# Graph attention with edge features on one core: one 384-element iota of GpSimd behind each batch of gathers, or one 128-element iota behind each gather

## The chip, the cores and the metric

The kernel runs on one core of a Trainium2 chip. Times are device microseconds of one execution. Where a profile is read, times are counted from the first instruction of the profiled execution, and "the span" is the time from its first to its last instruction. The engines are TensorE (PE; its weight loads are shown apart as PEld), VectorE (DVE), ScalarE (ACT), GpSimd (POOL) and SyncE (SP). Only the SP, ACT and POOL queues issue DMAs here.

## The reference

A graph has 6250 nodes with 128 features each and 206250 directed edges (200000 of them drawn in both directions, plus one self loop for each node). The edges are sorted by their destination. Each edge has 128 features of its own.

```
Qh, Kh, Vh = h @ WQ, h @ WK, h @ WV          # (6250, 8 heads, 16)
Eh         = edge_attr @ WE                  # (206250, 8, 16)
score = sum over 16 of Kh[src] * Qh[dst] * Eh / 4
score = exp(clip(score, -5, 5))
msg   = Vh[src] * score
h_out = segment_sum(msg, dst) / (segment_sum(score, dst) + 1e-6)
out   = layernorm(x + h_out)
```

The part that matters here is `Kh[src]` and `Vh[src]`: for every edge a row of 256 floats (K and V side by side) has to be fetched by its source node, and sources come in no order.

## The kernel before, in words

**Tiles and batches.** The edges are cut into `NT` = 1612 tiles of 128 (the last is partly padding). `cut_batches` groups them in 406 batches: 401 batches of `B` = 4 tiles, then five small ones that hold the last eight tiles (2, 2, 2, 1, 1).

**The table and the gathers.** At the start, the kernel writes the table `kv` (6250 rows of 256 floats) to HBM: `table` multiplies the nodes by `wkv`. From then on, `gather` (L304 to L320) fetches, for each tile, one row of 256 floats for each of the 128 edges, with one indirect DMA that GpSimd issues (L311) into a slot of the buffer `kvrows`. There are `GB` = 16 such buffers, one for a batch. The first `XB` = 12 batches can't wait for the table: they gather raw node rows from `x` (48 gathers) and multiply them by `wkv` later (`project`). Batches 12 to 405 gather from `kv`: 389 batches of four and five small ones, 1564 gathers.

**What GpSimd does beside gathers.** Behind the gathers of each batch from 12 on, GpSimd writes a row of 384 integers in each partition of a tile called `pause` (L319). Nothing reads that tile. It occupies GpSimd between the gathers of one batch and those of the next. Three other iotas run once, at the start: `io_i` (L118, 384 elements), `io2` (L121, 128 elements) and `third` (L138, one element).

**What sets the order.** From batch 12 on the instructions keep the order in which they are written (`manual_schedule`, L465). Each engine works through its own queue in order. In one turn of the loop (L463) GpSimd gets the gathers of batch b. The other engines work on several batches at once, each a stage further on: PE expands Q from a window of rows to the edges (`stage_a`, L353, into `qps`) and multiplies the edge features by `we` (L357); DVE multiplies the two (`pairs`, L364); PE transposes the product (`turn`, L372, into `pps`); DVE multiplies it by the gathered K (`stage_b`, L378, into `kq`), sums over 16 features (L381) and clips (L384); ACT takes the exponential (`weigh`, L390, L392); DVE multiplies the gathered V by it (`messages`, L412); PE sums the messages by destination with a one-hot matrix (`stage_c`, L430). The one-hot matrices come from DVE (`stage_0`, L339 and L343).

**What a gather waits for.** The gather for tile t waits for the landing of the gather eight earlier (GpSimd's DMAs go round eight semaphores). The first gather of a batch also waits until its buffer is free, which is after `messages` of the batch 16 earlier. And from batch `LOCK` = 20 on, the first gather of batch b waits for Q's expansion of batch b - 2 (L314 to L317). That dependency is in both kernels.

Of the kernel before, what the change touches and what calls it, by code (L numbers as in the profile page):

```python
# [15 lines left out]
P = 128  # L16
# [12 lines left out]
XB = 12  # L29
# [51 lines left out]
def edge_attention(ctx: ExitStack, tc: tile.TileContext, x, xT, srcT, dstT, dstB, dst0, bnd, lo, eaT,  # L81
                   wq, wkv, we, out, kv, qtab, qs, relD):
    nc = tc.nc
# [25 lines left out]
    def src_col(t):  # L109
        return src_sb[0][:, t:t + 1] if t < C0 else src_sb[1][:, t - C0:t - C0 + 1]  # L110

    with ExitStack() as fast:
# [6 lines left out]
        pause = ip.tile([P, 3 * P], I32, name="pause")  # L119
# [184 lines left out]
        def gather(b):  # L304
            rows, f = (x, D) if b < XB else (kv, 2 * D)
            g = gp.tile([P, B, 2 * D], F32, name="kvrows")
            for i, t in enumerate(batches[b]):
                k = min(P, (E - t * P + 63) // 64 * 64)
                if k < P:
                    nc.vector.memset(g[k:, i, :], 0.0)  # L310
                ins = nc.gpsimd.indirect_dma_start(  # L311
                    out=g[:k, i, :f], out_offset=None, in_=rows,
                    in_offset=bass.IndirectOffsetOnAxis(ap=src_col(t)[:k], axis=0))
                if i == 0 and b >= LOCK:  # L314
                    tc.add_manual_dep(ins.ins, expanded[b - STEP].ins.name,
                                      mybir.DependencyInfo(mybir.DependencyClass.Sync, mybir.DependencyReason.DATA),
                                      reason="gathers keep to TensorE's pace")  # L317
            if b >= XB:
                nc.gpsimd.iota(pause, pattern=[[1, 3 * P]], base=0, channel_multiplier=0)  # L319
            return g  # L320

        def project(g, n):
# [94 lines left out]
        def stage_c(b):  # L417
            n, g, oh, m = st8.pop(b)
            for i in range(n):
# [18 lines left out]
                elif last:  # L438
# [3 lines left out]
                    if k[1] == 0 and k[0] > 0:  # L442
                        ready.append(k[0] - 1)

        gathered = {b: gather(b) for b in range(min(XB, len(batches)))}
        for b0 in range(0, NB, KB):
            table(b0)
# [15 lines left out]
        for b in range(nbat + 4):  # L463
# [6 lines left out]
            if b < nbat:  # L470
                load_chunk(batches[b][0] // CH + EB - 3)
                load_rel(batches[b][0] // RC + 1)
                load_q(batches[b][0] // WT + QLOOK)
                g = gathered.pop(b) if b in gathered else gather(b)
                if b == min(XB, nbat - 1):
                    late_loads()
                if b == min(XB + 8, nbat - 1):
                    relative(C0, NT)
                if b == 14:
                    from_window(1)  # L480
                if b == 0:
                    for i in range(AHEAD):
                        stage_0(i)
                if b > 0:
                    turn(b - 1)
                stage_a(b, g)
            elif b == nbat:
                turn(b - 1)
# [178 lines left out]
```

## Time and profile before

| | |
|---|---|
| median of three runs | 2204.58 us (2202.32, 2204.58, 2208.21) |
| profiled execution | 2208.21 us, with a span of 2206.3 us |
| PE busy | 1468.0 us (67% of the span) |
| DVE busy | 1626.8 us (74%) |
| ACT busy | 478.9 us (22%) |
| POOL busy | 1719.4 us (78%), 2013 instructions |
| DMA | 398.18 MB, 180 GB/s on average |
| mean granted TensorE clock | 0.866 |

The busy share of an engine counts the time in which one of its instructions is shown as executing. A gather's bar on POOL shows GpSimd at work on it, not the transfer: the data lands later, and its landing is seen in what DVE waits for. The time that passes between two instructions of an engine with nothing to wait for is called "issue" by the profile. It isn't counted as busy, but the engine can't do anything else in it. So an engine can be without a moment to spare at a busy share well below 100%, and the way to see it is to look at what its waits are, not at the share.

### The profile page before, as it was taken

How to read it: one execution, taken by the hardware profiler on the slowest of the kernel's cores; microseconds unless marked ns; L12 is line 12 of the kernel's file. 1: busy time of each engine (PE TensorE's matmuls, PEld its weight loads, DVE VectorE, ACT ScalarE, POOL GpSimd, SP SyncE). 2: the span in 40 equal slices, each digit the busy share in tenths (PEclk: the TensorE clock that was granted, in tenths of full speed). 3: DMA queues.
4: the chain of work that ended last, by engine and by line, in shares of the span. 5: the costliest groups of instructions: out<-in, count | busy, mean ns of one | idle time of the engine just before them, and what ended most of it. 6: DMA issues, size and time to landing. Idle time of an engine off the chain costs nothing.

```text
span 2206.3 us, 25324 instructions
## 1 busy us (share of the span) xinstructions
PE 1468.0 (67%) x6880; PEld 1026.4 (47%) x6880; DVE 1626.8 (74%) x3779; ACT 478.9 (22%) x1572; POOL 1719.4 (78%) x2013
## 2 busy tenths in 40 slices
PE   6976666676666666666666666666766666666665
PEld 4754444454444444444444444444444444444443
DVE  3797778677777777777776776777777777777776
ACT  2522222222222221222221221222222211221211
POOL 7737777877777787787777778778778777777876
PEclk9998888878888998888888898998898888887888
DMA  8746555665566556555666556556655566656552
GB/s 283 247 135 203 173 183 160 192 193 163 171 188 193 180 163 199 177 182 161 181 188 181 181 168 201 179 163 191 186 181 163 177 192 181 181 165 200 176 161 78
DMA packets 178486, 398.18 MB, mean 180 GB/s; under 512 B 61757, under 2 KB 87527, under 8 KB 178337
## 3 DMA queue, kind: packets, MB, share of 16 engines
q0 software_dynamic: 76592, 208.18, 31.8%
q1 hardware_dynamic: 100604, 187.38, 27.2%
q8 instruction: 57, 0.93, 0.2%
q10 hardware_dynamic: 1140, 0.93, 0.1%
q14 instruction: 93, 0.75, 0.1%
HBM read 381.54 MB, written 14.81 MB: 180 GB/s over the span
## 4 chain that ended last, share of the span: by engine, by line
POOL 42%; DMA 21%; DVE 15%; issue 14%; PE 7%; POOLq 0%; ACT 0%; DVEq 0%; ACTq 0%; SPq 0%
POOL kvrows L311 39%; DMA kvrows<-kv,src 20%; POOL pause L319 4%; DVE kq L378 4%; DVE sc L381 3%; PE agg L430 2%; DVE msg L412 2%; DVE onehot L339 2%; PE eps L357 2%; DVE onehotT L343 1%; PE kvps L333 1%; PE pps L372 1%; DVE eq L364 1%; DMA kv<-kvst 1%; DVE sc L384 1%
## 5 line engine op out<-in xcount | busy, mean ns | idle before, releaser
L311 POOL DMA_INDIRECT kvrows<-kv,src x1564 | 1487.1, 951 | 453.1 <-issue 384.8
L430 PE MATMUL agg<-msg,onehot 128*128 128x136 f32 x3224 | 542.5, 318 | 605.0 <-DVE msg L412 295.4
L430 PEld LDWEIGHTS agg<-msg,onehot 128*128 128x128 f32 x3224 | 479.3, 218 | 916.7 <-issue 768.9
L378 DVE TENSOR_TENSOR kq<-kvrows,pps 128x512 f32<-128x512 f32 x406 | 276.3, 680 | 472.6 <-DMA kvrows<-kv,src 468.5
L357 PE MATMUL eps<-ea,we_sb 128*128 128x512 f32 (+1 forms) x812 | 487.9, 686 | 0.7 <-ACT kvrows L334 0.7
L372 PE MATMUL pps<-shift,eq 128*128 128x128 f32 x1612 | 310.2, 324 | 98.3 <-DVE eq L364 85.9
L355 ACT COPY qT<-qps 128x512 f32<-128x512 f32 x406 | 236.7, 583 | 587.1 <-PE qps L353 586.8
L372 PEld LDWEIGHTS pps<-shift,eq 128*128 128x128 f32 x1612 | 214.2, 163 | 155.8 <-DVE eq L364 150.0
L364 DVE TENSOR_TENSOR eq<-qT,eps 128x512 f32<-128x512 f32 x406 | 272.4, 671 | 18.9 <-PE eps L357 16.2
L381 DVE TENSOR_REDUCE sc<-kq 128x32 f32<-128x512 f32 x406 | 276.0, 680 | 7.3
L390 ACT ACTIVATE bank<-sc 128x32 f32<-128x32 f32 x406 | 81.8, 201 | 918.5 <-DVE onehot L339 911.8
L412 DVE TENSOR_TENSOR msg<-kvrows,bank 128x512 f32<-128x512 f32 x406 | 274.5, 676 | 5.6 <-ACT bank L390 5.5
L339 DVE TENSOR_TENSOR onehot<-bank,dst_sb 128x512 f32<-128x512 f32 x406 | 275.4, 679 | 0.0
L357 PEld LDWEIGHTS eps<-ea,we_sb 128*128 128x128 f32 x812 | 186.4, 231 | 31.6 <-ACT kvrows L334 3.2
L343 DVE TENSOR_SCALAR onehotT<-relb,node 126x512 bf16<-126x512 bf16 x406 | 192.7, 476 | 6.4 <-DMA relb<-relD 5.7
L319 POOL IOTA pause<- 128x384 int32 x394 | 185.3, 470 | 2.9
L353 PE MATMUL qps<-onehotT,qw 126*128 126x512 bf16 x406 | 183.2, 451 | 0.7 <-ACT qT L355 0.7
L384 DVE TENSOR_SCALAR sc<-sc 128x32 f32<-128x32 f32 x406 | 89.0, 219 | 7.3
L392 ACT ACTIVATE msg<-sc 128x32 f32<-128x32 f32 x406 | 86.5, 213 | 0.0
L400 PEld LDWEIGHTS finps<-sum,shift 128*128 128x128 f32 x478 | 64.5, 195 | 26.1 <-issue 25.9
L400 PE MATMUL finps<-sum,shift 128*128 128x136 f32 x478 | 64.4, 282 | 0.0
L311 POOL DMA_INDIRECT kvrows<-x,src x48 | 46.0, 958 | 16.2 <-issue 14.0
(67 smaller groups left out, 528.5 us busy)
## 6 DMA issues: line engine op xcount, KB each, us to landing
ea<-eaT SPq DMA_DIRECT2D x201, 512.0 KB
relb<-relD SPq DMA_DIRECT2D x100, 504.0 KB
kvrows<-kv,src POOLq DMA_INDIRECT x1564, 2.8
qw<-qs SPq DMA_DIRECT2D x202, 31.5 KB
kv<-kvst SPq DMA_DIRECT2D x12, 512.0 KB
qs<-qst SPq DMA_DIRECT2D x48, 96.0 KB
xb<-x SPq DMA_DIRECT2D x48, 64.0 KB
out<-h SPq DMA_DIRECT2D x48, 64.0 KB
```

The lines of the kernel that those rows point to most:

```text
L311: ins = nc.gpsimd.indirect_dma_start(out=g[:k, i, :f], out_offset=None, in_=rows, in_offset=bass.IndirectOffsetOnAxis(ap=src_col(t)[:k], a ...
L319: nc.gpsimd.iota(pause, pattern=[[1, 3 * P]], base=0, channel_multiplier=0)
L339: nc.vector.tensor_tensor(oh[:, :n], iota_p[:, None, :].to_broadcast([P, n, P]), rel[:, t0:t0 + n, None].to_broadcast([P, n, P]), op=ALU.i ...
L343: nc.vector.tensor_scalar(ohT[:, :n * P], rels[t0 // RC][:, e0:e0 + n * P], node[:QROWS], None, op0=ALU.is_equal)
L355: nc.scalar.copy(qT[:, :n * P], pq[:, :n * P])
L357: nc.tensor.matmul(pe[:, :n * P], we_sb, ea_tiles(t0, n), start=True, stop=True)
L364: nc.vector.tensor_tensor(eq[:, :n * P], qT[:, :n * P], pe[:, :n * P], op=ALU.mult)
L372: nc.tensor.transpose(pp[:, i, :], eq[:, i * P:i * P + P], ident)
L378: nc.vector.tensor_tensor(t1[:, :n], g[:, :n, :D], pp[:, :n], op=ALU.mult)
L381: nc.vector.tensor_reduce(sc[:, :n], t1[:, :n].rearrange("p b (h d) -> p b h d", h=H), axis=AX.X, op=ALU.add)
L412: nc.vector.tensor_tensor(m[:, :n, :D].rearrange("p b (h d) -> p b h d", h=H), g[:, :n, D:].rearrange("p b (h d) -> p b h d", h=H), exp_p[ ...
L430: nc.tensor.matmul(aggs[k], oh[:, i, :], m[:, i, :], start=first and not final, stop=last)
```

## The change

The iota behind each batch is taken out. Behind each single gather, from batch 12 on, GpSimd writes 128 integers in each partition of the same tile. A batch of four so has four iotas of 128 elements (512 elements in all) instead of one of 384; the small batches at the end have one for each of their gathers. GpSimd executes 1564 iotas instead of 394.

```diff
                 if i == 0 and b >= LOCK:
                     tc.add_manual_dep(ins.ins, expanded[b - STEP].ins.name,
                                       mybir.DependencyInfo(mybir.DependencyClass.Sync, mybir.DependencyReason.DATA),
                                       reason="gathers keep to TensorE's pace")
-            if b >= XB:
-                nc.gpsimd.iota(pause, pattern=[[1, 3 * P]], base=0, channel_multiplier=0)
+                if b >= XB:
+                    nc.gpsimd.iota(pause[:, :P], pattern=[[1, P]], base=0, channel_multiplier=0)
             return g
```

The instructions of PE, DVE, ACT and SP, and their order, stay as they are. No DMA is added, removed or moved.

## The prediction

> **What bounds the kernel now.** I read the waits first, because busy shares mislead here: POOL is busy 78% of the span, DVE 74%, PE 67%, and none looks full. The list of who waited for whom, restricted to GpSimd, has its causes on the right and total, number and longest wait behind the colon:
>
> ```profile
> POOL kvrows L311 <- issue: 398.8, 1428, 0.3
> POOL kvrows L311 <- DVE sc L384: 37.7, 26, 32.9
> POOL kvrows L311 <- DVE onehotT L343: 6.0, 33, 0.3
> POOL kvrows L311 <- DMA kvrows<-kv,src: 2.5, 11, 0.3
> ```
>
> The reader is to see the last column. With one exception no gather was ever held up by more than 0.3 us, and 0.3 us is what lies between any two gathers. The many small entries that name DVE, PE or a DMA are that same gap under another name. The exception is one wait of 32.9 us. GpSimd has nothing else to wait for, so outside that wait it is the bound, in spite of its 78%: 1719.4 busy, 453.1 + 16.2 idle before gathers, and 32.9 of that is the one real wait.
>
> The timeline of GpSimd (start, duration, instruction; in brackets the idle time before it) shows the rhythm, two batches of it:
>
> ```profile
> 155.89 0.47 POOL L319 IOTA pause<- 128x384 int32 x1
> 156.52 0.95 POOL L311 DMA_INDIRECT kvrows<-kv,src  x1 [0.16 <-DVE sc L381]
> 157.77 0.94 POOL L311 DMA_INDIRECT kvrows<-kv,src  x1 [0.30 <-issue]
> 159.02 0.95 POOL L311 DMA_INDIRECT kvrows<-kv,src  x1 [0.30 <-issue]
> 160.28 0.95 POOL L311 DMA_INDIRECT kvrows<-kv,src  x1 [0.30 <-issue]
> 161.24 0.46 POOL L319 IOTA pause<- 128x384 int32 x1
> 161.86 0.95 POOL L311 DMA_INDIRECT kvrows<-kv,src  x1 [0.16 <-DVE onehotT L343]
> ```
>
> From one batch to the next (156.52 to 161.86) it is 5.34 us, and near the end, at 2121.81 to 2127.15, it is 5.34 us again. Elsewhere the other engines wait for it. In the list of waits, DVE's greatest is for gathered rows:
>
> ```profile
> DVE kq L378 <- DMA kvrows<-kv,src: 468.5, 243, 6.2
> ```
>
> The one real wait stands in the early timeline:
>
> ```profile
> 106.13 0.47 POOL L319 IOTA pause<- 128x384 int32 x1
> 139.53 0.95 POOL L311 DMA_INDIRECT kvrows<-kv,src  x1 [32.94 <-DVE sc L384]
> ```
>
> Counting the gathers, this is the first gather of batch 20, where the wait for Q's expansion of batch b - 2 begins. In PE's timeline the expansion of batch 18 ends 0.27 us before 139.53, so that expansion is what it waited for. From then on the expansions pull ahead of the gathers, by a median of 14.0 us, since DVE needs only some 4 of each 5.34 us (518.33 busy of the 700 us from 700 to 1400). The last gather ends at 2191.67, and 14.6 us of PE and DVE work follow to the end of the span. So the end is set by: 139.53, plus 1531 steps of GpSimd from gather to gather, plus 15.6 us from the last gather's start.
>
> **The change, part by part.** The same 1532 gathers (batches 20 to 405) stay on that path. What changes is what stands between them.
>
> *What goes:* between the first gather of batch 20 and the last gather lie 385 iotas of 384 elements. What one costs is not its bar but what it adds from one gather's start to the next. Over the whole timeline a step without an iota takes 1.256 us (1218 steps) and one with an iota 1.590 us (without the 32.9 us wait). An iota adds 0.333 us: a gap of 0.01, a bar of 0.47 and a gap of 0.16, in place of a gap of 0.30. 385 x 0.333 = 128.2 us go.
>
> *What comes:* 1531 iotas of 128 elements, at c us each, 1531 c in all. Break-even is at c = 128.2 / 1531 = 0.084 us. The loop has no iota of 128, but the start of the program has one of each size, unobstructed:
>
> ```profile
> 0.86 0.44 POOL L118 IOTA io_i<- 128x384 int32 x1 [0.39 <-POOLq L655]
> 1.26 0.23 POOL L121 IOTA io<- 128x128 int32 x1
> 1.44 0.13 POOL L138 IOTA third<- 128x1 int32 x1
> ```
>
> There are three ways to c from these:
> - By the start spacings: 0.40 us from the start of the 384 to the next, 0.18 from the 128 to the next. 256 elements less save 0.22, so c = 0.333 - 0.22 = 0.113, and 1531 c = 173.0. Sum: +44.8 us.
> - By the difference of the bars: the groups give 439 and 227 ns, so c = 0.333 - 0.212 = 0.121, 185.3 us. Sum: +57.1.
> - By the bar alone with the gaps of the loop: 0.01 + 0.227 + 0.16 - 0.30 = 0.097, 148.5 us. Sum: +20.3.
>
> I take the first. The bars overlap here (the 384 starts at 0.86, lasts 0.44, and the next starts at 1.26), so a bar is longer than the time it keeps the engine, while a spacing from start to start has no such excess. The first way also gives 0.22 / 256 = 0.86 ns for an element, and 384 of those are 0.330 us, nearly the whole 0.333 measured in the loop. So an iota's fixed part appears to vanish in the 0.30 us that a gather needs anyway, and what counts is elements: 512 in a batch where there were 384. The third way leaves it open why the loop's bar is 470 ns where the start's is 439.
>
> The Trainium skill has a rule on this choice: "Perfetto Trace Analysis", section "GPSIMD Engine Instruction", says that a GpSimd instruction's bar is not to be relied on and that it should be timed by the start-to-start spacing of consecutive instructions. By that rule the sum is +44.8, by the bar alone +20.3.
>
> *The gap after the iota.* Only a batch's first gather has stood behind an iota so far, and it may wait for up to three semaphores; the others wait for one. Would theirs be another gap? Batches 13 to 15 answer it: their first gathers wait for one semaphore only (neither a buffer nor an expansion), and the gap is 0.16 there as well (69.35, 74.70, 80.05). Priced at nothing.
>
> *Held-up iotas.* 394 iotas have a median of 467 and a mean of 470 ns, so being held up costs 3 ns apiece. With 1531 in place of 385 that is up to 4.6 - 1.2 = 3.4 us more, at least nothing. I leave it out of the sum and add it to the upper end: +60.5. The Trainium skill ("SBUF — State Buffer", section "Who interferes with whom") speaks against more iotas in the same way: GpSimd shares its port pair with certain DVE operations, and whichever starts second is fully blocked. No run here shows what four times as many meetings cost.
>
> *Added waits.* Each iota waits for the one before it, since both write the same tile. A gather of 0.95 us lies between and covers it. [...]
>
> *The iotas of batches 12 to 19* add 32 x 0.113 - 8 x 0.333 = +1.0 us before the 32.9 us wait, which shrinks by as much. Cost nothing, up to 31 times this size. The gathers of batches 0 to 11 have no iota. The iota behind the very last gather delays nobody.
>
> *Other engines.* The order on SP and PE is unchanged, as it is on DVE and ACT apart from buffer numbers. No DMA moves to another queue or past another DMA. A gather waits for the landing of the one eight earlier, for which it has two batches, 10.7 us now and 10.9 then. Data for a batch is asked for later, DVE waits longer for it, and that wait grows without cost of its own.
>
> **Sum.** 2208.21 + 44.8 = 2253.0 for an execution like the profiled one. That one was 3.6 us above the median of the three runs (2204.58), so beside the median it is 2249.4. I say 2250 us, +2.0%.
>
> **The rivals.**
>
> *A. The short iota hides in the gap (faster).* Place: the 0.30 us between two gathers. Behind an iota the gap before the next gather is only 0.16, so 0.14 of the 0.30 can run beside something. If a 128-element iota kept the engine so briefly that c fell below 0.084, the change would gain. At c = 0.04 it is 61.2 - 128.2 = -67, 2138 us; at c = 0, the limit, -128, 2076. Against it: even the 227 ns bar with both known gaps gives 0.397, more than 0.30 by 0.097. The bar would have to fall under 0.214.
>
> *B. An iota has a large fixed price.* If nothing of it overlaps and its whole spacing of 0.18 us counts, then 1531 x 0.18 - 128.2 = +147, 2352 us. Against it: the 384-element one has a spacing of 0.40 at the start and adds only 0.333 in the loop, so some 0.07 does overlap.
>
> *C. The change moves nothing,* because landings or the expansions set the pace and GpSimd merely happens to fit: 2205 us. For it: DVE waits 468.5 us for landings, and these look like the bound. Against it: landings don't hold up the gathers, and a gather that starts later lands later.
>
> **How the numbers follow.** The forecast has 0.87, A 0.07, B 0.04, C 0.02. A's place is visible and the 128-element bar was seen only once, so it gets more than the others. The forecast's own bounds are +20.3 and +60.5, beside the median 2225 and 2265; the three runs spread 5.9 us around it, so I go 4 us beyond at both ends, 2221 to 2269. That leaves out A, B and C with 0.13 and a small rest. A measurement can tell about 0.3%, 6.6 us, from no change; all of the forecast and B lie above that, A mostly below the old time, C within. So faster 0.07, same 0.02, slower 0.91.
>
> **What would show it.** In the profile after: 1564 iotas with a bar of 0.23 to 0.26; a step from gather to gather of 1.37 us (1.256 + 0.113) where it was 1.25; 5.45 to 5.48 us a batch against 5.34; still no wait of GpSimd beyond its gaps except the one near 106 us, now about 32 us; DVE's wait for gathered rows up by some 40. It is wrong if the step is under 1.34 (A), over 1.42 (B), or if GpSimd has waits of several us at many batches (C).

## The result, and the profile after

The changed kernel takes 2271.3 us (median; 2268.9 to 2272.3), the kernel before beside it 2204.1 us. The ratio is 1.030, with a 95% interval from 1.028 to 1.032: 67 us slower, where +45 was forecast and the range ended at 2269. A second measurement gave 1.0298 (1.0281 to 1.0315). In some of the measurements below, every kernel, the one before included, took 2439 to 2484 us with TensorE as the bound (last section); a kernel is therefore always compared with the kernel before measured along with it.

GpSimd's waits in the changed kernel (total, number, longest):

```profile
POOL kvrows L311 <- issue: 249.0, 1446, 1.7
POOL kvrows L311 <- PE qps L353: 30.1, 6, 29.3
POOL kvrows L311 <- DVE h L605: 3.2, 20, 0.2
```

The large wait is the one at batch 20 (29.3 us). Otherwise GpSimd still waits for nobody on the path, so it is still the bound. (The program's very first gather waits 1.8 us for its indices, in both kernels; the prediction's "one exception" left that out, and it lies far ahead of the path.) New is the 1.7 behind "issue", where the longest was 0.3. GpSimd's timeline shows where such a time lies:

```profile
180.84 0.95 POOL L311 DMA_INDIRECT kvrows<-kv,src  x1 [0.16 <-issue]
181.79 0.26 POOL L319 IOTA pause<- 128x128 int32 x1
182.21 0.95 POOL L311 DMA_INDIRECT kvrows<-kv,src  x1 [0.16 <-PE agg L430]
183.17 0.25 POOL L319 IOTA pause<- 128x128 int32 x1
184.53 0.96 POOL L311 DMA_INDIRECT kvrows<-kv,src  x1 [1.11 <-issue]
185.50 0.25 POOL L319 IOTA pause<- 128x128 int32 x1
185.91 0.95 POOL L311 DMA_INDIRECT kvrows<-kv,src  x1 [0.16 <-issue]
```

A regular step is 1.37 us (180.84 to 182.21), with a gap of 0.16 behind the iota. From 183.42, where the bar of the iota ends, the gap is 1.11 us instead, and nothing the profile knows fills it. There are 15 such gaps, of 0.41 to 1.68 us, called stalls from here on. Less the regular 0.16 they are 10.1 us together. The groups of the iota, after and before (busy time, mean of one in ns, idle time before it):

```profile
L319 POOL IOTA pause<- 128x128 int32 x1564 | 398.1, 255 | 13.6
```

```profile
L319 POOL IOTA pause<- 128x384 int32 x394 | 185.3, 470 | 2.9
```

The start of the path moved as described, the wait absorbing what the early iotas cost:

```profile
107.56 0.25 POOL L319 IOTA pause<- 128x128 int32 x1
137.09 0.95 POOL L311 DMA_INDIRECT kvrows<-kv,src  x1 [29.27 <-PE qps L353]
```

And DVE's wait for gathered rows grew from 468.5 to 554.3 us, without being the cause of anything:

```profile
DVE kq L378 <- DMA kvrows<-kv,src: 554.3, 252, 7.0
```

**Where the 67 us are.** From the first gather of batch 20 to the start of the last gather, the profiled executions take 2051.2 us before (139.53 to 2190.76) and 2115.7 us after (137.09 to 2252.74): +64.4 us over 1531 steps. An iota of 128 adds, with the mean gaps and bars of the path (gap before the iota, its bar, regular gap behind it, less the gap between two bare gathers), 0.0087 + 0.2545 + 0.1609 - 0.3049 = 0.119 us. 1531 x 0.119 = 182.2; less the 128.2 that went, that is +54.0, and with 10.1 of stalls +64.1. The path begins 2.4 us earlier and its tail is 0.6 longer, which makes +62.6 for the span (2268.9 against 2206.3). The medians differ by 67, mainly because the profiled execution of the kernel before was its longest, 4.1 us above its median.

### The profile page after: what moved, and what is told of

The parts are those of the page before. It is cut to its first block, busy times and chain, and to the rows that moved or that the text cites. A ratio compares the mean times of both kernels' runs of the same rounds, so it can differ in the third digit from the quotient of the medians.

```text
span 2268.9 us, 26494 instructions
## 1 busy us (share of the span) xinstructions
PE 1498.1 (66%) x6880; PEld 1059.4 (47%) x6880; DVE 1590.2 (70%) x3779; ACT 479.6 (21%) x1572; POOL 1932.5 (85%) x3183
## 4 chain that ended last, share of the span: by engine, by line
POOL 46%; DMA 21%; DVE 14%; issue 10%; PE 8%; POOLq 0%; DVEq 0%; ACT 0%; SPq 0%; ACTq 0%
POOL kvrows L311 36%; DMA kvrows<-kv,src 19%; POOL pause L319 10%; DVE kq L378 4%; DVE sc L381 4%; PE agg L430 3%; PE eps L357 2%; DVE msg L412 1%; PE pps L372 1%; DVE onehot L339 1%; DVE eq L364 1%; PE kvps L333 1%; DMA kv<-kvst 1%; DVE sc L384 1%; DVE onehotT L343 0%
## 5 line engine op out<-in xcount | busy, mean ns | idle before, releaser
L430 PE MATMUL agg<-msg,onehot 128*128 128x136 f32 x3224 | 564.9, 327 | 680.0 <-DVE msg L412 330.5
L430 PEld LDWEIGHTS agg<-msg,onehot 128*128 128x128 f32 x3224 | 500.2, 226 | 993.1 <-issue 825.0
L378 DVE TENSOR_TENSOR kq<-kvrows,pps 128x512 f32<-128x512 f32 x406 | 276.2, 680 | 558.1 <-DMA kvrows<-kv,src 554.3
L357 PE MATMUL eps<-ea,we_sb 128*128 128x512 f32 (+1 forms) x812 | 494.7, 695 | 0.7 <-ACT kvrows L334 0.7
L319 POOL IOTA pause<- 128x128 int32 x1564 | 398.1, 255 | 13.6
L372 PE MATMUL pps<-shift,eq 128*128 128x128 f32 x1612 | 317.8, 330 | 53.7 <-DVE eq L364 47.0
L372 PEld LDWEIGHTS pps<-shift,eq 128*128 128x128 f32 x1612 | 223.3, 167 | 106.3 <-DVE eq L364 100.9
L343 DVE TENSOR_SCALAR onehotT<-relb,node 126x512 bf16<-126x512 bf16 x406 | 154.5, 381 | 6.0 <-DMA relb<-relD 5.3
L384 DVE TENSOR_SCALAR sc<-sc 128x32 f32<-128x32 f32 x406 | 94.6, 233 | 7.3
```

Of the source, the lines that this page charges most:

```text
L319: nc.gpsimd.iota(pause[:, :P], pattern=[[1, P]], base=0, channel_multiplier=0)
L357: nc.tensor.matmul(pe[:, :n * P], we_sb, ea_tiles(t0, n), start=True, stop=True)
L372: nc.tensor.transpose(pp[:, i, :], eq[:, i * P:i * P + P], ident)
L378: nc.vector.tensor_tensor(t1[:, :n], g[:, :n, :D], pp[:, :n], op=ALU.mult)
L430: nc.tensor.matmul(aggs[k], oh[:, i, :], m[:, i, :], start=first and not final, stop=last)
```

## The experiments

My theory: GpSimd's steps from gather to gather are the whole path, an iota costs about 0.8 ns an element and a small fixed part there, and the rest is the stalls. Its rivals: only elements count; the stalls come from the number of instructions, from the alternation of iota and gather, or from the longer step; and, without iotas, another bound takes over at once.

**The changed kernel again.**

> The changed kernel as it is, once more, beside the kernel before on the same chip. The first four variants ran on a chip on which the kernel before takes 2467 us where it took 2204 us in the runs of the prediction, with a granted TensorE clock of about 0.80 in place of 0.866, and GpSimd had waits at many batches there. Theory (where TensorE is granted less, it and DVE set the pace at some 6.0 us a batch, and GpSimd's 5.34 or 5.48 us don't reach the end): on that chip the changed kernel is within 0.6% of the kernel before, 2467 to 2482 us; on a chip with 0.866 it is 2.8 to 3.2% slower, 2270 us. Rival (the change costs its 64 us of GpSimd time on any chip): 2531 us on the slower chip.

Measured: 2273.7 us against 2207.5, ratio 1.0298 (1.0281 to 1.0315), with the 15 stalls at the same gathers as in the first profile. Laying the 2467 us to the chip, as I did there, was wrong: two of the chips gave both times.

**No iota at all.**

```diff
-            if b >= XB:
-                nc.gpsimd.iota(pause, pattern=[[1, 3 * P]], base=0, channel_multiplier=0)
```

> The iota behind each batch is taken out and none is put in. Theory (GpSimd's steps from gather to gather set the end, whatever fills them): the 385 iotas on the path cost 0.333 us each, so the time falls by 128 us to some 2076 us, and a step is 1.25 us throughout. Rival (GpSimd is the bound only because the pause makes it so; without it landings, buffers or Q's expansion hold the gathers back): the steps are 1.25 us, but waits of several us appear at first gathers of batches, and the time lies well above 2076, at 2120 to 2210 us.

> No iota at all, beside the kernel before. Two chips so far ran the kernel before in 2467 us, at 6.0 us a batch, and were indifferent to the iotas; one ran it in 2207 us. Theory, for a chip of the second kind (GpSimd's steps set the end down to the bare gathers): 2205 - 128 = 2077 us. Rival (the next bound takes over at once): 2120 to 2210 us, with waits of GpSimd at first gathers of many batches. On a chip of the first kind: 2467 us, as the kernel before.

Measured with TensorE as the bound: 2469.4 us against 2467.0, ratio 1.0009 (0.9999 to 1.0019), and 1.0012 on a repeat. Measured otherwise: 2079.5 us against 2208.7, ratio 0.942 (0.940 to 0.943). The forecast of the theory was 2077. GpSimd's waits of that execution show no new bound:

```profile
POOL kvrows L311 <- issue: 375.4, 1231, 0.3
POOL kvrows L311 <- PE qps L351: 39.4, 15, 35.1
POOL kvrows L311 <- DVE sc L382: 27.1, 89, 0.3
```

Apart from the wait at batch 20, now 35.1 us, there is no gap above 0.3 on the path. So the gathers alone, at 1.256 us each, still set the end, and the rival falls. This kernel is 6% faster than the kernel before; where TensorE is the bound it takes the same time.

**One iota of 512 elements behind each batch:** the elements of the changed kernel in the instructions of the old one.

```diff
-        pause = ip.tile([P, 3 * P], I32, name="pause")
+        pause = ip.tile([P, 4 * P], I32, name="pause")
...
-                nc.gpsimd.iota(pause, pattern=[[1, 3 * P]], base=0, channel_multiplier=0)
+                nc.gpsimd.iota(pause, pattern=[[1, 4 * P]], base=0, channel_multiplier=0)
```

> One iota of 512 elements behind each batch: as many elements in a batch as the changed kernel has, in as many instructions as the kernel before had. Theory (an iota costs its elements at 0.83 ns, plus a small fixed part, and the stalls of up to 1.7 us that the changed kernel shows every 146 us come with its 1170 more instructions): an iota adds 0.333 + 0.106 = 0.44 us, the time is 2204 + 385 x 0.106 = 2245 us, and there are no stalls. Rival (only elements count; the stalls come from the extra time between gathers): about 2271 us, as the changed kernel.

> One iota of 512 elements behind each batch, beside the kernel before, for a chip on which that takes some 2205 us. Theory (0.83 ns an element, stalls with the number of instructions): the iota adds 0.333 + 0.106 = 0.44 us, the time is 2207 + 385 x 0.106 = 2248 us, ratio 1.019, and GpSimd has no stall above 0.33 us beside the one wait. Rival (the 512 elements are the whole price, however they are cut): 2271 us, ratio 1.030. Second rival (stalls come from the longer time between batches, not from the number of instructions): 2258 us, with stalls.

Measured with TensorE as the bound: 1.0000 (0.9991 to 1.0010), repeated 1.0013. Measured otherwise: 2243.4 us against 2202.7, ratio 1.0195 (1.0174 to 1.0215), and no stall. The group in that profile:

```profile
L319 POOL IOTA pause<- 128x512 int32 x394 | 227.8, 578 | 2.8
```

The bar is 108 ns longer than with 384 elements, 0.84 ns an element. The mean step over the path is 1.365 us against 1.340: 1531 x 0.025 = 38 us for 385 x 128 elements, 0.78 ns an element. So the same 512 elements cost 41 us in one piece and 67 in four. The difference is the stalls (10) and what an iota costs beside its elements.

**An iota of 96 elements behind each gather:** the elements of the old kernel in the instructions of the changed one.

```diff
-                    nc.gpsimd.iota(pause[:, :P], pattern=[[1, P]], base=0, channel_multiplier=0)
+                    nc.gpsimd.iota(pause[:, :96], pattern=[[1, 96]], base=0, channel_multiplier=0)
```

> An iota of 96 elements behind each gather: 384 elements in a batch, as before, in four instructions instead of one. Theory (elements at 0.83 ns, a fixed part, stalls with the number of instructions): the step is 1.37 - 0.027 = 1.343 us, 1531 x 0.092 - 128 = +13 us, and about 15 stalls with 10 us in all stay, so 2227 us. Rival (only elements count): 2204 us, and no stalls.

> An iota of 96 elements behind each gather, beside the kernel before, for a chip on which that takes some 2205 us: 384 elements in a batch, in four instructions instead of one. Theory (0.83 ns an element, a fixed part that the gap doesn't hide wholly, stalls with the number of instructions): a step of 1.343 us, 1531 x 0.092 - 128 = +13 us, and some 10 us of stalls, 15 of them at about 146 us from one another, and 5 us of held-up iotas, together +25 to +28 us, ratio 1.0125. Rival (elements alone count): ratio 1.000. Second rival (stalls need the longer step of the 128 elements): ratio 1.008, no stalls.

Measured with TensorE as the bound: 1.0049 (1.0032 to 1.0066), repeated 1.0051. Measured otherwise: 2230.8 us against 2204.4, ratio 1.0121 (1.0103 to 1.0140); the theory had said 1.0125. The step is 1.34 us, and there are 15 stalls (10.8 us), in time 143 us apart where they were 146, and counted in gathers from the program's first at the very same ones: the 114th gather, then every 106th from there.

**An iota of one element behind each gather.**

```diff
-                    nc.gpsimd.iota(pause[:, :P], pattern=[[1, P]], base=0, channel_multiplier=0)
+                    nc.gpsimd.iota(pause[:, :1], pattern=[[1, 1]], base=0, channel_multiplier=0)
```

> An iota of one element behind each gather, where the kernel before takes some 2205 us. Theory (an iota of one element adds 0.012 us to a step; the stalls come with an iota behind every gather, at gathers 114, 220, 326 and so on): 2080 + 18 + 10 = 2108 us, ratio 0.956, with 15 stalls. Rival (no stalls, since the step is nearly that of bare gathers): 2098 us, ratio 0.951. Rival (one element hides wholly): 2080 us, ratio 0.943.

Measured: 2115.1 us against 2201.9, ratio 0.960 (0.959 to 0.962). GpSimd's timeline:

```profile
501.76 0.96 POOL L311 DMA_INDIRECT kvrows<-kv,src  x1 [0.16 <-issue]
502.73 0.14 POOL L319 IOTA pause<- 128x1 int32 x1
503.03 0.96 POOL L311 DMA_INDIRECT kvrows<-kv,src  x1 [0.16 <-issue]
504.00 0.14 POOL L319 IOTA pause<- 128x1 int32 x1
```

The iota with its gaps fits almost exactly into the 0.30 us that lie between two bare gathers: 0.01 + 0.14 + 0.16 = 0.31. But the gather's own bar is 0.96 where it was 0.95. Over the path a step is 1.280 us against 1.256 without iotas, and 15 stalls of 12.6 us in all account for 0.008 of that. The fixed price of an iota is so 0.016 us, 24 us over the path, and most of it (0.010) is in the gather's bar (mean 961 ns against 951). So the 0.30 us that the profile calls "issue" is not time in which the engine can do nothing else, as I had put it ahead of the prediction: nearly a whole one-element iota fits in. The stalls need no elements. With TensorE as the bound this kernel was 1.0036 to 1.0046 times as long as the kernel before.

**Four iotas of 96 elements together, behind each batch:** as many instructions as in the changed kernel, without the alternation.

```diff
             if b >= XB:
-                nc.gpsimd.iota(pause, pattern=[[1, 3 * P]], base=0, channel_multiplier=0)
+                for j in range(4):
+                    nc.gpsimd.iota(pause[:, 96 * j:96 * j + 96], pattern=[[1, 96]], base=0, channel_multiplier=0)
```

> Four iotas of 96 elements behind each batch, one after the other, in place of one of 384: as many elements as before, as many instructions as the changed kernel has, but three of four gathers still follow a gather directly. Theory (the stalls come at fixed places of GpSimd's program, with the number of its instructions): 15 stalls of 0.4 to 1.7 us, about 26.5 batches apart, 10 us in all; the three more iotas cost their fixed part (start spacings of 0.40 us for 384 elements and 0.18 us for 128 give 0.07 us each, 3 x 0.07 x 385 = 81 us), so 2205 + 91 = 2296 us, ratio 1.041, on a chip on which the kernel before takes some 2205 us. Rival (the stalls come because every gather stands behind an iota): no stalls, 2286 us, ratio 1.037. Second rival (the fixed part hides, elements alone count): 2205 to 2215 us.

> Four iotas of 96 elements behind each batch, once more, to be read where the kernel before takes some 2205 us. In the run above each four of them kept GpSimd for 0.70 us in place of 0.47, and the step around them was 1.83 us in place of 1.59. Theory (stalls at fixed places of GpSimd's program, with the number of instructions): 385 x 0.24 = +92 us and 15 stalls of 10 us in all, 26.5 batches apart, ratio 1.046. Rival (stalls come because every gather stands behind an iota): no stalls, ratio 1.042.

Measured with TensorE as the bound: 0.9996 (0.9986 to 1.0006). Measured otherwise: 2306.7 us against 2208.5, ratio 1.0450 (1.0432 to 1.0467). By the time alone it could be either; the list of waits decides, where on the path nothing but the wait at batch 20 exceeds 0.3 us:

```profile
POOL kvrows L311 <- issue: 390.8, 1367, 0.3
POOL kvrows L311 <- DVE sc L385: 33.6, 15, 30.6
```

So the number of instructions doesn't make the stalls. It also shows that an iota behind another iota adds more than one behind a gather: 384 elements in four pieces keep GpSimd for 0.70 us in place of 0.47, some 0.08 us for each further iota, where a short iota between two gathers has a fixed price of 0.016.

**The changed kernel with one iota of one element more behind each batch.**

```diff
                 if b >= XB:
                     nc.gpsimd.iota(pause[:, :P], pattern=[[1, P]], base=0, channel_multiplier=0)
+            if b >= XB:
+                nc.gpsimd.iota(pause[:, P:P + 1], pattern=[[1, 1]], base=0, channel_multiplier=0)
```

> The changed kernel with one iota of one element more behind each batch: one instruction more in a batch, nearly no elements. Where the kernel before takes some 2205 us: the additional iota costs at most its start spacing of some 0.1 us, 385 x 0.1 = 38 us, so 2271 to 2310 us. What it tells: the stalls of the changed kernel are 106 gathers (26.5 batches) apart. Theory (their places go by GpSimd's instructions): with some tenth more instructions in a batch they are 94 to 98 gathers apart. Rival (they go by the number of gathers): 106 gathers again. Second rival (they need a batch of nothing but pairs of gather and iota): none.

Measured: 2446.2 us against 2446.3, ratio 1.0003 (0.9990 to 1.0015), with TensorE as the bound, so its time says nothing on GpSimd. Its stalls can still be read at gathers that aren't the first of a batch, since those have no wait for Q's expansion: gathers 220, 326, 432, 644, 750, 856 and on to 1492, the numbers of the changed kernel, though there is a tenth more instructions in a batch. (At 114, 538 and 1598, where the batch's first gather had been held up by 1.3 to 1.4 us, the gap is only 0.29.) The theory of the fixed place in the program falls: the place goes by the number of gathers. Here is the one at gather 326:

```profile
554.59 0.96 POOL L311 DMA_INDIRECT kvrows<-kv,src  x1 [0.16 <-issue]
555.56 0.25 POOL L319 IOTA pause<- 128x128 int32 x1
557.43 0.95 POOL L311 DMA_INDIRECT kvrows<-kv,src  x1 [1.61 <-issue]
```

**One iota of 384 elements behind a batch's first gather** in place of its last, so that it stands directly ahead of every second place of a stall.

```diff
-            if b >= XB:
-                nc.gpsimd.iota(pause, pattern=[[1, 3 * P]], base=0, channel_multiplier=0)
+                if i == 0 and b >= XB:
+                    nc.gpsimd.iota(pause, pattern=[[1, 3 * P]], base=0, channel_multiplier=0)
             return g
```

> One iota of 384 elements in a batch, as before, but behind the batch's first gather in place of its last. Counting gathers, the stalls of every kernel so far that shows any stand at gather 114 and every 106 gathers from there (114, 220, 326, ...), also with one more instruction in a batch; these are by turns the second and the fourth gather of a batch. Theory (the place goes by the number of gathers, and the stall shows where an iota stands directly ahead of that gather): now 7 or 8 stalls of about 1.1 us at the second gathers of batches (gathers 114, 326, 538, 750, ...), none at 220, 432, ..., and with 2205 us for the kernel before 2212 us, ratio 1.003 to 1.005. Rival (stalls need an iota behind every gather): no stalls, ratio 1.000.

Measured: 2203.5 us against 2203.6, ratio 1.0000 (0.9991 to 1.0010), and no stall. GpSimd's waits below the one at batch 20:

```profile
POOL kvrows L311 <- issue: 316.8, 1221, 0.3
POOL kvrows L311 <- DMA kvrows<-kv,src: 51.5, 171, 0.3
```

My theory of the stall falls in its second half too: one iota directly ahead of the gather isn't enough. Nor does it matter for the time whether the iota stands behind a batch's first gather or its last.

**The kernels side by side,** where GpSimd was the bound (mean step over the path; stalls with their sum):

| iotas in a batch of four | us | before, us | ratio (95%) | step, us | stalls |
|---|---|---|---|---|---|
| none | 2079.5 | 2208.7 | 0.942 (0.940 to 0.943) | 1.256 | none |
| 1 element behind each gather | 2115.1 | 2201.9 | 0.960 (0.959 to 0.962) | 1.280 | 15, 12.6 us |
| 384 behind the first gather | 2203.5 | 2203.6 | 1.000 (0.999 to 1.001) | 1.337 | none |
| 96 behind each gather | 2230.8 | 2204.4 | 1.012 (1.010 to 1.014) | 1.354 | 15, 10.8 us |
| 512 behind the batch | 2243.4 | 2202.7 | 1.020 (1.017 to 1.022) | 1.365 | none |
| 128 behind each gather (the change) | 2271.3 | 2204.1 | 1.030 (1.028 to 1.032) | 1.382 | 15, 10.1 us |
| 4 x 96 behind the batch | 2306.7 | 2208.5 | 1.045 (1.043 to 1.047) | 1.405 | none |

Each time follows from its step: 1531 steps and some 154 us ahead and behind (1531 x 1.256 + 154 = 2077; x 1.382 + 154 = 2270).

## Why the prediction was right and wrong

- **The bound was right.** GpSimd, busy 78%, sets the end; a change of its step appears in the time in full, in both directions, from 1.256 to 1.405 us. Rival C is refuted in these executions. In those of 2439 to 2484 us it is C's picture that holds: the first gathers wait for TensorE, and the variants take 0.9996 to 1.0051 times as long as the kernel before. The changed kernel itself was not measured there, only with one more iota of one element (1.0003).
- **What went was right:** 0.333 us for each of the 385. Taking them out without replacement shortened the path from 2051.2 to 1922.8 us, by 128.4, where 128.2 had been worked out.
- **The step that failed is "the gap after the iota ... priced at nothing".** The regular gap is 0.16 at every gather, as argued from batches 13 to 15. But in 15 places it is 0.41 to 1.68 us, and that is 10 us. The trace of before has no gap of that kind, and three gaps that were read there couldn't bound what an iota behind every gather would bring up.
- **A second term was mis-sized: the price of a short iota, by the coarseness of the rows.** Of the three ways I took the start spacings (c = 0.113). Measured is 0.119, 9 us more over the path. The way was right, but the rows show hundredths of a microsecond. The trace itself has the three starts at 0.857, 1.256 and 1.441 us; the spacings are 0.399 and 0.185, their difference is 0.214 and not 0.22, and c = 0.333 - 0.214 = 0.119, the measured value. The changed kernel's rows of the same three iotas start at 0.85, 1.25 and 1.44, and would have given c = 0.123. The second way (0.121) came close because the groups give nanoseconds.
- **Held-up iotas add little.** Their mean bar is 255 ns against a median of 250, 5 ns apiece where 3 had been seen: 2 ns more, 3 us over the path. The 0.333 that c starts from is a mean and has the 3 in it, so the upper end of the sum counted them twice.
- **Either miss alone would have left the time inside the range; stalls and price together put it 2 us outside.** Even the upper end of the sum, +60.5, was below the 64.4 on the path. The correction of 3.6 us for a long profiled execution added to the miss, and 2253 would have been the nearer figure; where in the program that execution lost its 4 us is not shown.
- **Rivals A and B.** A is refuted: 128 elements cost 0.119 us, above the break-even of 0.084. The overlap that A built on is real, though: all but 0.016 us of the one-element iota disappears in the gap. B, which had the whole 0.18 count, is refuted by the same 0.119.
- **The signs.** 1564 iotas of 0.25 us, a step of 1.37, 5.48 us a batch, a shorter wait at batch 20 and 86 us more waiting of DVE came as described (for the last, 40 was said). That GpSimd would have no gap beyond its regular ones did not.
- **The Trainium skill's rule** ("Perfetto Trace Analysis", section "GPSIMD Engine Instruction") to time GpSimd by start spacings and not by the bar agrees with these runs: the unrounded spacings give 0.119, the measured price, while the bar alone, as seen at the start of the program, had given 0.097. What failed was the rounding of the starts, not the rule.

**What stays open.** What the stall is. Its place goes by the number of gathers, whatever the number of instructions, and it needs no elements. Where GpSimd was the bound, it showed with an iota behind each gather and not with one or four iotas in one place of a batch. But the iotas alone don't make it, as the executions with TensorE as the bound show. In the kernel without any iota, gathers 325 and 326, and gathers 537 and 538, each time a batch's first gather and the one behind it:

```profile
558.81 0.95 POOL L311 DMA_INDIRECT kvrows<-kv,src  x1 [1.86 <-PE agg L428]
560.32 0.94 POOL L311 DMA_INDIRECT kvrows<-kv,src  x1 [0.57 <-issue]
```

```profile
868.84 0.94 POOL L311 DMA_INDIRECT kvrows<-kv,src  x1 [0.30 <-PE agg L428]
870.09 0.94 POOL L311 DMA_INDIRECT kvrows<-kv,src  x1 [0.30 <-issue]
```

Both second gathers have numbers of the list (114, 326, 538, ...). Where the batch's first gather had been held up, the gap is 0.57 in place of 0.30; where it had not, nothing is to be seen. It is so without exception in the five such executions of the kernels with no iota, with 512 elements and with 4 x 96 behind the batch: of 40 second gathers with numbers of the list, the 19 behind a held-up first gather (by 0.4 us or more) have gaps of 0.56 to 0.66, the other 21 the regular 0.30. And in all twenty profiles, from batch 12 to 400, no gap above 0.35 stands at any other gather that isn't the first of its batch. So something happens at these gathers without an iota behind every gather too, and whether it shows depends on what stands ahead of them. Why an iota behind every gather brings it up, and why it then costs most at a second gather whose first was not held up, is not shown.

## What to carry to other kernels

An engine whose waits never exceed its regular gap is the bound, at whatever busy share, and any filler in its queue costs what it adds to a step, times its count; the first thing to try is to take the filler out. Price a small instruction by what it adds between its neighbours, not by its bar, and from figures as fine as the count asks for: 0.006 us at 1531 places are 9 us, so rows in hundredths need a range to match. Give the sum a term for irregular gaps when an instruction is added at over a thousand places. And look at which engine is the bound in the execution at hand: the same pause was worth 128 us in one kind of run and nothing in another.

## What the runs showed of the hardware that I had not expected

- GpSimd's stall every 106 gathers, above.
- A kernel can change its bound from one measurement to the next. In the runs of 2439 to 2484 us the mean granted TensorE clock is 0.79 to 0.81 in place of 0.84 to 0.88. For the kernel before it is some 7% lower there, while the time is 11 to 12% longer. And TensorE's results arrive long after the end that the profile models for them. In the kernel with 512 elements, PE's and DVE's timelines while the table is built:

```profile
28.70 1.22 PE L233 MATMUL kvacc<-wkv_sb,xT_sb 128*128 128x256 f32 x2 [6.25 <-issue]
33.65 1.22 PE L233 MATMUL kvacc<-wkv_sb,xT_sb 128*128 128x256 f32 x2 [3.73 <-issue]
38.49 1.22 PE L233 MATMUL kvacc<-wkv_sb,xT_sb 128*128 128x256 f32 x2 [3.62 <-issue]
```

```profile
33.17 0.42 DVE L236 COPY kvst<-kvacc 128x256 f32<-128x256 f32 x1 [12.00 <-remote]
```

The matmuls are shown as done at 29.92, and DVE's copy of their result, which waits for TensorE's semaphore alone, starts at 33.17. In the profile's windows the granted clock is 0.50 from 30 to 70 us. In the loop, a batch then takes 5.85 us, and GpSimd is held up at 117 first gathers by 0.4 to 2.8 us, at nearly all of them last by TensorE's semaphore. The 512 elements cost nothing there (1.0000). What takes TensorE's speed in those runs is not shown; the same chips gave both kinds of run.
- In those runs, an iota behind every gather still cost 0.4 to 0.5%, with one element as with 96, while 128 elements with one more iota cost nothing (1.0003). What makes the difference is not shown.
